# Three raw windows instead of two, an earlier start of the edge gathers, and another pace of the expert work

## The chip, the cores and the metric

The kernel runs on one core of a Trainium2 chip. The metric is the device time of one execution in microseconds (us); the median of three runs before the change is 1178.66 us (1176.34 to 1180.91). The engines are TensorE (PE, with its weight loads as PEld), VectorE (DVE), ScalarE (ACT), GpSimd (POOL) and SyncE (SP). Each works through its own queue in the order of the program and waits at semaphores for the others. DMAs are issued from the queues of SP, ACT and POOL.

## What is computed

A graph layer and a mixture of experts over 6250 nodes of 256 numbers, with 100000 edges sorted by their target:

```python
x = x + gnn(layernorm(x), stack([src, dst]), W, b)
x = x + ffn(layernorm(x)[None], ...)[0]

# gnn
msg_sum = segment_sum(h[src], dst)
deg = segment_sum(ones, dst)
return concat([h, msg_sum / maximum(deg, 1)], 1) @ W.T + b

# ffn: two of eight experts for every node
xn = layernorm(x) * gamma + beta
w = softmax over the two largest of xn @ Wr + br
for e in range(8):
    h = gelu(xn @ W1[e] + b1[e])
    y += (h @ W2[e] + b2[e]) * w[e]
```

## The kernel before

**Two products ahead of the edges.** W has two halves. The z part (`z_block`, 13 blocks of four node tiles) multiplies the normalized nodes by the half for neighbours and stores z in DRAM (`z_d`); eight more columns carry the router. The own half, u, is made in 25 steps (`u_stages`, two node tiles each) later, between edge tiles, and is stored in `u_d`.

**The edge loop.** The edges are cut into 56 windows (W) of 14 tiles (C) of 128 edges; t = 14 g + c counts the 784 edge tiles. `gather` (L646) is an indirect DMA on POOL's queue: 128 rows of z into one of 28 buffers `xg` (XG). `add_edges` (L665) multiplies seven tiles at a time (HC) by one-hot matrices `hot` into the PSUM tile pS, of which there is one; the two halves of its partitions take every second tile. It is called at c = 6 and c = 13, and the gathers for the tile 28 further on follow it, since they reuse the buffers. So a gather needs the matmul of the tile 28 before it.

**Raw windows.** The first two windows (RAW) do not wait for z. `gather_raw` (L345) loads the source indices `src_i` on SP and gathers rows of x itself; `raw_statistics`, `raw_deviations` (DVE) and `scale_raw` (ACT, L329) normalize them, seven tiles at a time; after the sum `take_raw_sums`, `turn_raw_sums` and `multiply_raw_sums` copy, transpose and multiply the window's sums by the weights. `gather_raw` is called at the sixth block of z. What else is to be done in the z part stands in the list `steps`, two entries a block from the fourth block on. Window 0's first half is normalized there; its edges are added in the edge loop at t = 0 and 7. Window 1 is normalized at t = 2 and t = 15.

**A window's end.** `window_done` (L1062) sets by tile counts what follows: `keep_sums` copies pS (ACT, L692), which frees it for the next window; `merge_sums` (PE, L696) makes pX; `window_x1` (DVE) divides by the degree and adds u, which `load_u` fetches by a load on SP at a row that a register holds. For the last window, whose rows would run over the end of u_d, `load_last` (L707) fetches u by an indirect DMA on POOL, with indices from `place_tail`. Four windows make a group: it is normalized, routed, sorted by expert and planned, with offsets in tiles from the classes Steps, LateSteps and LastSteps. The plan (which rows of y_d belong to a node) is stored by `put_plan` on SP.

**Experts.** 60 tiles after a group's end (36 and 29 in the late ones) its expert tasks are ready: per pair of experts two `hidden` steps counted as 2.0 us and two `result` steps counted as 1.75 us, 30 us for a group. `after` (L1133) lets out so much of them per edge tile: 0.72, in the last 56 tiles 0.6, after the edges 1.2 or 2.0. Three batches of 8, 5 and 1 groups (BATCHES) have 8, 5 and 2 spare tiles (`more_stages`) for tokens beyond an expert's slots.

**The end.** When a batch is complete, `gather_rows` loads x1 on SP and gathers each node's two rows of y_d on POOL, into the same 28 buffers; `add_rows` (DVE, L1031) weighs and adds them and stores the result from SP. These gathers stand behind all edge gathers on POOL.

Everything is in an order that the program writes out (`manual_schedule`): no engine reorders it.

Of the kernel before, what the change touches and what calls it, by code (L numbers as in the profile page):

```python
# [8 lines left out]
F32 = mybir.dt.float32  # L9
I32 = mybir.dt.int32  # L10
# [13 lines left out]
CAP = 64  # L24
BATCHES = (8, 8), (5, 5), (1, 2)
GB = 3
LATE = 40
XG = 28
RAW = 2
LATE_CHUNKS = 4  # L30
# [3 lines left out]
def gnn_ffn_kernel(ctx: ExitStack, tc: tile.TileContext, x, x_cols, src, dst, dst_next, gw, gw_t, gb, gb_cols, gamma, beta,  # L34
# [73 lines left out]
    z_d = dram.tile([HR, DZ], F32, name="z_d")  # L108
    u_d = dram.tile([HR, DZ], F32, name="u_d")
    y_d = dram.tile([batches[-1].end_row, D], F32, name="y_d")  # L110
# [59 lines left out]
    dst_i = u_pool.tile([P, W, C], I32, name="dst_i", bufs=1)  # L170
    xg = [edges.tile([P, DA], F32, name=f"xg{i}") for i in range(XG)]

    def constants():
        for g in xg:
            nc.vector.memset(g[:, D:DZ], 0.0)
            nc.vector.memset(g[:, DZ:], 1.0)
        nc.vector.tensor_scalar(before, ej, 0.0, None, op0=ALU.is_lt)
        nc.scalar.activation(cols, coli, AF.Copy)
        nc.vector.tensor_copy(lane, lanei)
        nc.vector.tensor_scalar(upper, col, lane, None, op0=ALU.is_gt)  # L180
        nc.vector.tensor_scalar(second, lane, HALF - 0.5, None, op0=ALU.is_gt)
        nc.vector.scalar_tensor_tensor(lane_of, second, -float(HALF), lane, op0=ALU.mult, op1=ALU.add)
# [135 lines left out]
    def raw_statistics(some):  # L318
        for t in some:
            statistics(mv_e[:, t, :], xg[t][:, :D])  # L320

# [5 lines left out]
    def scale_raw(some):  # L327
        for t in some:
            nc.scalar.activation(xg[t][:, :D], xg[t][:, :D], AF.Identity, scale=rstd_e[:, t:t + 1])  # L329

# [11 lines left out]
    def load_edges():  # L342
        nc.sync.dma_start(dst_i, dst)

    def gather_raw():  # L345

        nc.sync.dma_start(src_i, src)
        for t in range(RAW * C):
            nc.gpsimd.indirect_dma_start(  # L349
                out=xg[t][:, :D], out_offset=None, in_=x[:, :],  # L350
                in_offset=bass.IndirectOffsetOnAxis(ap=src_i[:, t // C, t % C:t % C + 1], axis=0))
# [18 lines left out]
    ends = edges.tile([P, W], F32, name="ends")  # L370
    tail_i = edges.tile([P, 1], I32, name="tail_i")
    wrongs = const.tile([1, 1], F32, name="wrongs")
# [27 lines left out]
    def place_edges():  # L400
# [4 lines left out]
            [P, W, HC, 2]), op=ALU.subtract)  # L405

    def place_tail():
        tail_f = early.tile([P, 1], F32, name="tail_f", bufs=1)
        nc.vector.tensor_tensor(tail_f, bases[:, 0, W - 1:W], lane, op=ALU.add)
        nc.vector.tensor_scalar(tail_f, tail_f, float(N - 1), None, op0=ALU.min)  # L410
        nc.vector.tensor_copy(tail_i, tail_f)

# [84 lines left out]
    hot_first = u_pool.tile([P, C, HALF], F32, name="hot_first", bufs=1)  # L497
    zero = u_pool.tile([CAP, D], F32, name="zero", bufs=1)

    def clear_first():  # L500
        nc.vector.memset(zero, 0.0)
        nc.vector.memset(states, 0.0)

    def make_hot(hot, g, c):
        nc.vector.tensor_tensor(hot, cols[:, None, :HALF].to_broadcast([P, HC, HALF]),  # L505
                                rel[:, g, c:c + HC, None].to_broadcast([P, HC, HALF]), op=ALU.is_equal)

    steps = [[constants], [lambda: placed_rows.append(place_windows())], [lambda: router_columns(0)],
             [lambda: spread_windows(placed_rows[0])], [lambda: wide_b.append(router_biases())],
             [lambda: center_weights(0)], [place_rows, place_tail], [lambda: add_biases(wide_b[0])], [place_edges],  # L510
             [lambda: make_hot(hot_first[:, :HC], 0, 0)], [check_windows], [lambda: make_hot(hot_first[:, HC:], 0, HC)], [],
             [clear_first], [some(raw_statistics, 0, 3)],
             [some(raw_statistics, 3, 2)], [some(raw_statistics, 5, 2), lambda: raw_deviations(0, HC)],
             [some(scale_raw, 0, HC), some(raw_statistics, HC, 3)], [some(raw_statistics, HC + 3, HC - 3)]]
    router_weights()
# [15 lines left out]
    for t0 in blocks:  # L531
        if t0 + 4 * TB in blocks:
            load_block(t0 + 4 * TB)
        if t0 == blocks[5]:
            gather_raw()
        z_block(t0, steps if t0 >= blocks[3] else None)
    assert not ahead
    assert not steps
    raw_deviations(HC, C - HC)
    scale_raw(range(HC, C))  # L540
    u_tasks = u_stages()
# [9 lines left out]

    loads = [(b1_sb, b1), (b2_sb, all_rows(b2, [[D, NX], [1, D]]))]

# [92 lines left out]
    def gather(g, c):  # L646
        nc.gpsimd.indirect_dma_start(  # L647
            out=xg[(g * C + c) % XG][:, :DZ], out_offset=None, in_=z_d[:, :],
            in_offset=bass.IndirectOffsetOnAxis(ap=src_i[:, g, c:c + 1], axis=0))
# [7 lines left out]
    def merge_tiles(V):  # L657
# [3 lines left out]
        if V.g > 0:  # L661
            V.carry = work.tile([P, HALF], F32, name="carry")
            nc.vector.tensor_scalar(V.carry, cols[:, :HALF], 0.0, ends[:, V.g - 1:V.g], op0=ALU.is_equal, op1=ALU.mult)

    def add_edges(V, first, last):  # L665
        if first == 0:
            V.pS = ps.tile([P, DA], F32, name="pS", bufs=1)
        halves = V.pS[:HALF, :], V.pS[HALF:, :]
        for c in range(first, last):
            nc.tensor.matmul(halves[c % 2], V.hot[c // HC][:, c % HC, :], xg[(V.g * C + c) % XG],  # L670
                             start=(c < 2), stop=(c >= C - 2 and (c % 2 == 1 or V.g == 0)))
        if last == C and V.g > 0:
            nc.tensor.matmul(halves[0], V.carry, V.before.raw if V.g < RAW else V.before.sums, start=False, stop=True)  # L673

# [23 lines left out]
    def load_u(V):  # L698
        if V.g < W - 1:
            V.x1 = work.tile([P, DZ], F32, name="x1", bufs=CW)  # L700
            nc.sync.dma_start(V.x1, u_d[window_rows(V.g), :])
        else:
            V.x1 = u_last

    u_last = edges.tile([P, DZ], F32, name="u_last")

    def load_last():  # L707
        nc.gpsimd.indirect_dma_start(
            out=u_last, out_offset=None, in_=u_d[:, :],
            in_offset=bass.IndirectOffsetOnAxis(ap=tail_i, axis=0))  # L710

# [298 lines left out]
    def spare():  # L1010

        nonlocal spares
        spares += 1
        return xg[(W * C + spares - 1) % XG][:, :D]

# [25 lines left out]
    class Steps:  # L1041

        x1, var, roots, norms, route, exps, weigh, choices, count = 3, 5, 7, 9, 11, 14, 15, 16, 19
        hot, sort = (22, 24, 26, 28), (26, 28, 30, 32)
        runs, rest, place, tiles, copied, rows, pace, start, apart = 30, 33, 36, 39, 40, 46, 1.5, 60, 2

    class LateSteps:

        x1, var, roots, norms, route, exps, weigh, choices, count = 3, 4, 5, 7, 9, 11, 12, 13, 15
        hot, sort = (17, 18, 20, 22), (19, 21, 23, 25)  # L1050
        runs, rest, place, tiles, copied, rows, pace, start, apart = 20, 22, 24, 27, 26, 28, 1.25, 36, 1

    class LastSteps:

        x1, var, roots, norms, route, exps, weigh, choices, count = 3, 4, 5, 6, 7, 8, 9, 10, 12
        hot, sort = (13, 14, 17, 18), (15, 16, 19, 20)
# [5 lines left out]
    def window_done(V, G, K, t):  # L1062
# [10 lines left out]
        at(t + more, keep_sums, V)  # L1073
        at(t + more + S.x1 - 1, merge_sums, V)
        at(t + S.x1 + more, window_x1, V)
# [57 lines left out]
    def after(t):  # L1133
# [6 lines left out]

        pace = 0.6 if W * C - 56 <= t < W * C else 0.72 if t < W * C else 1.2 if len(Ks) < W // CW else 2.0
        spent = min(spent + pace, pace) if tasks else 0.0
# [7 lines left out]
    def new_window(g, V_before):  # L1150
        V = Group()
        V.g, V.before, V.hot = g, V_before, []
        if g == 0:
            V.hot = [hot_first[:, :HC], hot_first[:, HC:]]
        else:
            hot_tiles(V, 0)
        merge_tiles(V)
        return V

    def groups(g):  # L1160

        if g == 0:
            return {0: (0, HC), HC: (HC, C)}
        if g == W - 1:
            return {HC - 1: (0, HC), C - 4: (HC, C - 3), C - 1: (C - 3, C)}
        return {HC - 1: (0, HC), C - 1: (HC, C)}

    now = 0
    V = new_window(0, None)
    edge_tiles = [(g, c) for g in range(W) for c in range(C)]  # L1170
    for g, c in edge_tiles[RAW * C:XG]:
        gather(g, c)
# [3 lines left out]
    for index in range(W // CW):  # L1176
# [10 lines left out]
        for g in range(K.first, K.first + CW):  # L1187
            if g > 0:
                V = V_next
            for c in range(C):  # L1190
# [5 lines left out]
                if c == 0 and g > 0:  # L1196
                    hot_tiles(V, HC)
                if t in (2, C + 1):
                    some_raw = range(C, C + HC) if t == 2 else range(C + HC, 2 * C)
                    raw_statistics(some_raw)  # L1200
# [4 lines left out]
                if some_edges:  # L1205
                    for g_c in edge_tiles[g * C + some_edges[0] + XG:g * C + some_edges[1] + XG]:
                        gather(*g_c)
                for to, what in loads[:1]:
                    loads.pop(0)
                    nc.sync.dma_start(to, what)  # L1210
                if u_tasks and t >= HC and t % 3 == 0:
                    u_tasks.pop(0)()
                    if not u_tasks:
                        u_pools.close()
                        slots = fast_pools.enter_context(tc.tile_pool(name="slots", bufs=2))
                        at(t + 60, load_last)
                        xe = slots.tile([P, KD, SC], F32, name="xe", bufs=1)
# [168 lines left out]
```

## Time and profile before

| What | us |
|---|---|
| median of three runs | 1178.66 |
| the profiled execution | 1180.93 |
| its span (first to last instruction) | 1178.8 |
| first raw gather on POOL | 46.5 |
| last store of z issued on SP | 72.4 |
| last edge gather starts | 1031.4 |
| last gather of y_d starts | 1166.1 |

The table by stretches of the trace (us; busy time and instructions of each engine, granted clock of PE, share of the 16 DMA engines, GB/s):

```profile
30.00:60.00 30.00, 28.09 (x133) 23.24 (x131) 26.20 (x128) 11.47 (x28) 10.48 (x11) 1.00 1.00 391
120.00:150.00 30.00, 27.63 (x144) 18.40 (x144) 21.10 (x63) 2.27 (x4) 22.99 (x24) 1.00 0.86 272
500.00:600.00 100.00, 86.80 (x503) 62.12 (x504) 48.49 (x198) 41.40 (x116) 75.64 (x81) 0.97 0.55 138
1050.00:1100.00 50.00, 37.99 (x127) 26.77 (x128) 33.72 (x119) 20.64 (x65) 31.40 (x33) 0.83 0.66 174
```

The five figures with an x are PE, PEld, DVE, ACT and POOL. In a timeline a row gives the start, the duration, the engine and line, the operation with its output and inputs, how often, and in brackets how long the engine sat idle before it and what ended that. A queue's row (SPq) is the issue of a DMA, not its transfer.

### The profile page before, as it was taken

The page shows a single profiled execution, that of the slowest core. Times are in us where ns is not written, and L with a number is a line of the kernel's source. Part 1 is how long each engine was busy: PE and PEld are TensorE (multiplying, and loading weights), DVE is VectorE, ACT ScalarE, POOL GpSimd, SP SyncE. Part 2 cuts the span into 40 slices and gives each one's busy share as a digit, 9 for nine tenths or more (in the row PEclk, how much of TensorE's full clock was granted, in tenths as well). Part 3 has the DMA queues.
Part 4 walks back from the last instruction along what each step waited for, and adds up shares of the span by engine and source line. Part 5 has one row for each costly group of instructions (what it writes and reads, how often), then busy time and mean ns, then how long its engine had stood idle before and what let it go on. Part 6 is the DMA issues. An engine that isn't in the chain of part 4 may idle for free. (4 is left out here: it accounts for less than half of the span.)

```text
span 1178.8 us, 19193 instructions
## 1 busy us (share of the span) xinstructions
PE 973.3 (83%) x5470; PEld 717.0 (61%) x5470; DVE 650.6 (55%) x2530; ACT 477.2 (40%) x1305; POOL 845.1 (72%) x892
## 2 busy tenths in 40 slices
PE   7967974897989788897979889899889989888960
PEld 5745652776757465574747567467676767665840
DVE  5887694554546364544635545374644636267442
ACT  2441017444454344445334434445364524434410
POOL 0377777777777777777777777777777777777674
PEclk9998987898989799998979979999999999989985
DMA  9988878966565655556565555755665564767784
GB/s 318 395 259 271 281 237 250 282 172 135 144 136 141 146 139 140 141 136 136 143 138 138 148 125 145 147 144 138 160 128 154 134 156 135 170 195 186 228 239 115
DMA packets 128859, 210.04 MB, mean 178 GB/s; under 512 B 36652, under 2 KB 87064, under 8 KB 128620
## 3 DMA queue, kind: packets, MB, share of 16 engines
q0 software_dynamic: 42768, 118.85, 42.3%
q1 hardware_dynamic: 77644, 80.45, 21.0%
q10 hardware_dynamic: 8336, 9.45, 2.5%
q8 instruction: 46, 0.75, 0.3%
q14 instruction: 65, 0.53, 0.1%
HBM read 163.80 MB, written 44.86 MB: 177 GB/s over the span
## 5 line engine op out<-in xcount | busy, mean ns | idle before, releaser
L647 POOL DMA_INDIRECT xg<-z_d,src_i x756 | 719.1, 951 | 230.6 <-issue 121.5
L670 PE MATMUL pS<-xg,hot 128*64 128x265 f32 x1540 | 267.6, 417 | 54.9 <-DMA xg<-z_d,src_i 54.4
L932 PEld LDWEIGHTS ph<-xe,w_sb 128*128 128x128 f32 x1792 | 223.4, 202 | 15.4 <-issue 9.2
L932 PE MATMUL ph<-xe,w_sb 128*128 128x128 f32 x1792 | 228.6, 287 | 2.3 <-ACT xe L905 2.3
L670 PEld LDWEIGHTS pS<-xg,hot 128*64 128x64 f32 x1540 | 122.8, 142 | 172.6 <-DMA xg<-z_d,src_i 95.5
L945 PE MATMUL py<-w_sb,hid 128*128 128x256 f32 x896 | 219.1, 392 | 9.7 <-DVE rows L949 6.1
L945 PEld LDWEIGHTS py<-w_sb,hid 128*128 128x128 f32 x896 | 168.0, 193 | 50.0 <-issue 16.8
L937 ACT ACTIVATE hid<-ph,b_sb 128x128 f32<-128x128 f32 x448 | 127.1, 368 | 141.4 <-PE ph L932 141.1
L905 ACT ACTIVATE xe<-xs x448 | 139.4, 311 | 77.5 <-ACT xe L905 37.6
L949 DVE TENSOR_TENSOR rows<-py,b_sb 128x512 f32<-128x512 f32 x56 | 38.6, 689 | 169.6 <-PE py L945 168.1
L1024 POOL DMA_INDIRECT xg<-y_d,plans x98 | 97.1, 991 | 38.4 <-issue 16.8
L764 ACT ACTIVATE xs<-pm,beta_sb,gamma_sb 128x256 f32<-128x256 f32 x112 | 57.1, 568 | 112.4 <-PE pm L761 112.4
L696 PE MATMUL pX<-sums,merge 128*128 128x265 f32 x112 | 41.7, 457 | 51.5 <-ACT sums L692 51.5
L714 DVE TENSOR_SCALAR rdeg<-pX 128x1 f32<-128x1 f32 x56 | 8.6, 153 | 134.9 <-PE pX L696 134.9
L692 ACT ACTIVATE sums<-pS 128x265 f32<-128x265 f32 x56 | 21.7, 388 | 139.2 <-PE pS L673 133.7
L505 DVE TENSOR_TENSOR hot<-cols,rel 128x448 f32<-128x448 f32 x110 | 67.3, 612 | 10.0 <-PE pS L670 10.0
L349 POOL DMA_INDIRECT xg<-x_dram,src_i x28 | 26.7, 954 | 52.8 <-DMA src_i<-src_dram 44.6
L281 PE MATMUL ph<-gc,x_t 128*128 128x264 f32 (+1 forms) x200 | 58.3, 416 | 6.4 <-ACT zt L305 3.5
L761 PE MATMUL pm<-to,xn 128*128 128x256 f32 x224 | 58.6, 393 | 5.7 <-DVE to L754 3.5
L1031 DVE SCALAR_TENSOR_TENSOR xg<-xg,plans,xg 128x256 f32<-128x256 f32 (+1 forms) x98 | 46.4, 483 | 28.3 <-DMA xg<-y_d,plans 26.8
L696 PEld LDWEIGHTS pX<-sums,merge 128*128 128x128 f32 x112 | 20.3, 206 | 66.8 <-ACT sums L692 65.1
L937 ACT ACT_TABLE_LOAD x25 | 32.1, 1283 | 62.1 <-PE ph L932 57.6
(229 smaller groups left out, 1069.4 us busy)
## 6 DMA issues: line engine op xcount, KB each, us to landing
y_d<-rows SPq DMA_DIRECT2D x56, 256.0 KB
xg<-z_d,src_i POOLq DMA_INDIRECT x756, 3.3
w_sb<-w_dram ACTq DMA_DIRECT2D x16, 512.0 KB
x<-u_d SPq DMA_DIRECT2D x55, 132.0 KB
x_d<-x SPq DMA_DIRECT2D x55, 128.0 KB
u_d<-u_t SPq DMA_DIRECT2D x24, 264.0 KB
x_t<-x_cols_dram SPq DMA_DIRECT2D x12, 512.0 KB
xu<-x_dram SPq DMA_DIRECT2D x24, 256.0 KB
```

What stands on the lines that cost most here:

```text
L281: nc.tensor.matmul(pz, x_t[:, t, k, :], gc[:, h * KD + k, :n], start=(k == 0), stop=(k == KD - 1))
L505: nc.vector.tensor_tensor(hot, cols[:, None, :HALF].to_broadcast([P, HC, HALF]), rel[:, g, c:c + HC, None].to_broadcast([P, HC, HALF]), op ...
L647: nc.gpsimd.indirect_dma_start(out=xg[(g * C + c) % XG][:, :DZ], out_offset=None, in_=z_d[:, :], in_offset=bass.IndirectOffsetOnAxis(ap=sr ...
L670: nc.tensor.matmul(halves[c % 2], V.hot[c // HC][:, c % HC, :], xg[(V.g * C + c) % XG], start=(c < 2), stop=(c >= C - 2 and (c % 2 == 1 or ...
L696: nc.tensor.matmul(V.pX, V.merge, V.sums, start=True, stop=True)
L761: nc.tensor.matmul(px[:, k, :], G.xn[i][:, k * P:(k + 1) * P], G.one_hot[i], start=True, stop=True)
L764: nc.scalar.activation(xs[:, at:at + 2 * P], px[:, k, :], AF.Identity, bias=beta_sb[:, k:k + 1], scale=gamma_sb[:, k:k + 1])
L905: nc.scalar.activation(xe[:, :, bass.ds(to_at, CAP)], src[:, :, bass.ds(src_at, CAP)], AF.Copy)
L932: nc.tensor.matmul(ph[:, i, a * SH:(a + 1) * SH], w1_sb[:, U.e + a, k, c * P:(c + 1) * P], xe[:, k, at:at + SH], start=(k == 0), stop=(k = ...
L937: nc.scalar.activation(U.hid[:, c, a * SH:(a + 1) * SH], ph[:, i, a * SH:(a + 1) * SH], AF.Gelu, bias=b1_sb[:, U.e + a, c:c + 1])
L945: nc.tensor.matmul(U.py[:, h, :], U.hid[:, c, h * P:(h + 1) * P], w2_sb[:, U.e + h, c, :], start=(c == 0), stop=(c == KH - 1))
L1024: nc.gpsimd.indirect_dma_start(out=V.y2[r], out_offset=None, in_=y_d[:K.batch.end_row, :], in_offset=bass.IndirectOffsetOnAxis(ap=plans[:c ...
```

## The change

- RAW is 3: 42 raw tiles. They need 42 buffers: 14 more (`third`) lie in the pool of the u part. `rows_for` gives a tile's buffer: the first 28 tiles and all from tile 42 on use the 28 buffers, tiles 28 to 41 use `third`.
- `gather_raw` is called at the third block of z (`blocks[2]`) and loads only the first three windows' indices; the other 53 follow at the eighth block (`load_sources`).
- All 14 tiles of window 0 are normalized and summed in the z part: `add_edges` stands in `steps`, twice. The check of the windows moves behind it.
- In the edge loop windows 1 and 2 are normalized at t = 2, 15, 23 and 29. The first 14 gathers of z (window 3) are issued at the start; windows 0 and 2 are followed by none, window 1 by those of tiles 56 to 69; from window 3 on it is 28 tiles ahead again.
- The expert pace is 0.95 on all edge tiles, and the middle batch has 4 spare tiles for 5.
- `merge_sums` has an offset of its own, one tile later than before except in the last group.
- u_d has 128 more rows, which are cleared, so the last window loads its u on SP like all others. `place_tail` and `load_last` are gone.
- The buffers are one tile, and its constant columns are set by four wide memsets in place of 56.

```diff
-BATCHES = (8, 8), (5, 5), (1, 2)
+BATCHES = (8, 8), (5, 4), (1, 2)
-RAW = 2
+RAW = 3
...
+    def rows_for(t):
+        if XG <= t < RAW * C:
+            return third[:, t - XG, :]
+        return xg[(t if t < XG else t - RAW * C) % XG]
...
+    def load_sources():
+        nc.sync.dma_start(src_i[:, RAW:], src[:, RAW:])
...
-        nc.sync.dma_start(src_i, src)
+        nc.sync.dma_start(src_i[:, :RAW], src[:, :RAW])
...
-             [lambda: make_hot(hot_first[:, :HC], 0, 0)], [check_windows], [lambda: make_hot(hot_first[:, HC:], 0, HC)], [],
-             [clear_first], [some(raw_statistics, 0, 3)],
-             [some(raw_statistics, 3, 2)], [some(raw_statistics, 5, 2), lambda: raw_deviations(0, HC)],
-             [some(scale_raw, 0, HC), some(raw_statistics, HC, 3)], [some(raw_statistics, HC + 3, HC - 3)]]
+             [lambda: make_hot(hot_first[:, :HC], 0, 0)], [lambda: make_hot(hot_first[:, HC:], 0, HC)],
+             [some(raw_statistics, 0, 4)], [some(raw_statistics, 4, HC - 4), lambda: raw_deviations(0, HC)],
+             [some(scale_raw, 0, HC), some(raw_statistics, HC, 2)],
+             [lambda: add_edges(V_first, 0, HC), some(raw_statistics, HC + 2, 3)],
+             [some(raw_statistics, HC + 5, C - HC - 5), lambda: raw_deviations(HC, C - HC)],
+             [some(scale_raw, HC, C - HC), clear_first], [lambda: add_edges(V_first, HC, C), check_windows], []]
...
-        if t0 == blocks[5]:
+        if t0 == blocks[2]:
             gather_raw()
+        if t0 == blocks[7]:
+            load_sources()
...
-        at(t + more + S.x1 - 1, merge_sums, V)
+        at(t + more + S.merge, merge_sums, V)
...
-        pace = 0.6 if W * C - 56 <= t < W * C else 0.72 if t < W * C else 1.2 if len(Ks) < W // CW else 2.0
+        pace = 0.95 if t < W * C else 1.2 if len(Ks) < W // CW else 2.0
...
+    raw_at = {2: C, C + 1: C + HC, C + HC + 2: 2 * C, 2 * C + 1: 2 * C + HC}
...
-                if t in (2, C + 1):
-                    some_raw = range(C, C + HC) if t == 2 else range(C + HC, 2 * C)
+                if t in raw_at:
+                    some_raw = range(raw_at[t], raw_at[t] + HC)
...
-                    for g_c in edge_tiles[g * C + some_edges[0] + XG:g * C + some_edges[1] + XG]:
-                        gather(*g_c)
+                    ahead = XG if g >= RAW else RAW * C if g * C < XG else None
+                    if ahead:
+                        for g_c in edge_tiles[g * C + some_edges[0] + ahead:g * C + some_edges[1] + ahead]:
+                            gather(*g_c)
...
-                        at(t + 60, load_last)
```

## The prediction

> **What bounds the kernel now.** First the busy times, then GpSimd's (POOL's) timeline, since the issue time between slices is not counted as busy.
>
> ```profile
> PE 973.3 (83%) x5470; PEld 717.0 (61%) x5470; DVE 650.6 (55%) x2530; ACT 477.2 (40%) x1305; POOL 845.1 (72%) x892
> ```
>
> PE looks fullest. POOL's timeline (start, duration, line, idle before it and releaser) says otherwise:
>
> ```profile
> 46.47 1.13 POOL L349 DMA_INDIRECT xg<-x_dram,src_i  x1 [44.62 <-DMA src_i<-src_dram]
> 47.91 0.98 POOL L349 DMA_INDIRECT xg<-x_dram,src_i  x1 [0.31 <-issue]
> ...
> 172.82 0.94 POOL L647 DMA_INDIRECT xg<-z_d,src_i  x1 [0.30 <-DMA xg<-z_d,src_i]
> ...
> 1031.43 0.95 POOL L647 DMA_INDIRECT xg<-z_d,src_i  x1 [0.30 <-issue]
> 1032.68 0.95 POOL L1024 DMA_INDIRECT xg<-y_d,plans  x1 [0.30 <-issue]
> ...
> 1086.63 0.94 POOL L1024 DMA_INDIRECT xg<-y_d,plans  x1 [1.00 <-DVE of L838]
> 1087.88 0.94 POOL L1024 DMA_INDIRECT xg<-y_d,plans  x1 [0.30 <-issue]
> 1091.49 0.94 POOL L1024 DMA_INDIRECT xg<-y_d,plans  x1 [2.67 <-DMA out_dram<-xg]
> 1092.74 0.95 POOL L1024 DMA_INDIRECT xg<-y_d,plans  x1 [0.30 <-issue]
> 1099.50 0.94 POOL L1024 DMA_INDIRECT xg<-y_d,plans  x1 [5.82 <-DVE xg L1031]
> ```
>
> A gather takes 0.95 us and the next starts 0.30 after it: pitch 1.25. From 46.47 to 1032.68 stand 785 gathers (784 tiles, one last u); 785 x 1.25 = 981 of 986 us. POOL never waits for a buffer there. Then come 98 gathers of y_d (122 us) with a hole at 1085 to 1099 (0.70 + 2.37 + 5.52 = 8.6 us over the usual 0.30), and 12.7 us from the last gather's start (1166.1) to the end. So the end moves with POOL's chain. Gather n+28 needs the buffer of tile n, so I looked for how far PE is ahead of that, in PE's timeline:
>
> ```profile
> 98.27 3.13 PE L670 MATMUL pS<-xg,hot 128*64 128x265 f32 x14
> 114.39 2.00 PE L670 MATMUL pS<-xg,hot 128*64 128x265 f32 x14
> 126.43 2.00 PE L670 MATMUL pS<-xg,hot 128*64 128x265 f32 x14
> 167.04 2.88 PE L670 MATMUL pS<-xg,hot 128*64 128x265 f32 x14
> ```
>
> These are the first matmuls of tiles 14, 28, 42 and 70. Tile 70 at 167.0 frees the buffer for gather 98, at 172.8: slack 5.8 us; for tile 42 it is 10.0 (gather 70 starts at 136.4), from tile 168 on 20 to 28. Here PE does not wait for gathers (tile 70's ended 30 us earlier); it waits for DVE and ACT:
>
> ```profile
> 75.27 0.11 DVE L639 MEMSET xs<- 128x64 f32 x1 [0.86 <-DMA z_d<-zt]
> ...
> 75.53 0.42 DVE L201 BATCH_NORM_STATS2 st<-xg 128x6 f32<-128x256 f32 x1
> 75.98 0.18 DVE L202 BATCH_NORM_AGGREGATE mv_e<-st 128x2 f32<-128x6 f32 x1
> ...
> 80.71 0.17 DVE L196 TENSOR_TENSOR rstd_e<-rstd_e,newton 128x7 f32<-128x7 f32 x1
> ```
>
> Seven raw tiles hold DVE 5.4 us (75.5 to 80.9), and ACT 2.9 us to scale them (L329). The raw part of a window is dear on DVE, not on POOL.
>
> **The change, part by part.** *Earlier raw gathers.* The first src load stands on SP behind the loads of block 6 (x_t issued at 22.95) instead of 36.38. From issue to first gather took 9.2 us (37.23 to 46.47); the same again gives a start at 23.4 + 9.2 = 32.6, 13.9 us earlier. 42 raw gathers then last to 85.1, by which time z lies in DRAM (below: 79.6), so POOL goes on without a hole up to gather 56.
>
> In 30 to 60 us the table by stretches shows a DMA share of 1.00 at 391 GB/s. Eleven gathers of 131 KB brought forward are 1.44 MB, 3.7 us at that rate, by which the x loads of the z part may come later. I take 0 for it, since DVE's only wait for an x tile after 25 us is 0.79 and the loads run four blocks ahead; 3.7 is the upper bound. A rule speaks against the change here: the Trainium skill (DMA: Bandwidth & Descriptors, Issuing engines are not separate DMA queues) says that the DMAs of all issuers interleave on the same 16 engines, so that a transfer from POOL takes from one of SP; by it the 3.7 would be paid in full, and the sum below would end 3.7 higher, at 1190.
>
> *Window 0 inside the z part.* DVE's work from the first hot tiles (51.56) to the second raw deviations (74.3) is 22.7 us. Without the window check and the clears (2.9), moved behind it, 19.9 remain, begun 1.4 earlier (1.0 of memsets made wide, 0.4 of the tail): 70.0. Then in order: scale 2.9 on ACT, 14 edge matmuls 2.0, the last z product 0.9, its scale 0.5: 76.3, against 72.4. The store took 2.9 to free DVE's first instruction of the main loop: 79.2, and with hand-overs of 0.1 each 79.6, 4.3 later.
>
> *Third raw window: two more DVE blocks of 5.4.* From 75.3 to 93.7 DVE ran 18.5 us of things that stay, so window 1's second statistics end at 98.1; scale 2.9 and copy 0.4 free the PSUM: window 1 starts on PE at 101.7 (was 98.3). Its edges 3.1, merge 0.6, four u products 3.7, second edges 1.9: 111.0. Now a new wait: the instruction order puts the first scaling of window 2 ahead of the copy of window 1's sums on ACT. DVE: two u steps at 1.8, hot and merge tiles 1.2, u after its products (107.9), x1 1.5, statistics 5.4: 114.8; ACT 2.9 + 0.4: 118.1. Behind the copy on PE stand the transposes and all that follows. DVE: two u steps and hot tile 4.2, statistics 5.4: 124.4; scale and the keep of window 1 (queued behind it): 127.8. Window 2 starts at 127.9 (was 114.4). Then edges 1.9, merge 0.6, four products 3.7, edges 1.9, u 1.9, transposes, copy and multiply 1.9, u 1.9: tile 42 at 141.7, 15.3 late. From tile 42 to 70 PE took 40.6, set by u stores and the first routing on DVE; nothing there becomes shorter: tile 70 at 182.3.
>
> So the 13.9 us gained are lost again at gather 70 (142 instead of 136.4), and gather 98 goes at 182.4 instead of 172.8: **+9.6**. Bounds: below, DVE without a pause from 79.6 has 51 us ahead of tile 42's u products (four raw blocks 21.6, eleven u steps 19.8, hot tiles, checks and two x1 9.6): 131, 4.6 late, within tile 70's slack of 5.8, so 0; above, 3.7 for the x loads and 2 for hand-overs that I have cut too short, +15.3.
>
> *Expert pace 0.95 for 0.72.* In the first group the new order has four expert steps of 1.9 us more ahead of tile 140: 7.6. Tile 140: 248.5 + 15.3 + 7.6 = 271.4; gather 168 is ready at 261.6 + 9.6 - 1.25 (the last u's gather, gone from in front of it) = 270.0. **+1.5**, and **-1.25** for the u gather. The load takes 0.35 on SP and adds its zeroes in a 0.4 us issue, both beside POOL. Later groups have 20 us of slack against 8. Bounds 0 and +4.
>
> *Tail.* Group 12's experts get 0.95 for 0.6 in the last 20 tiles, 7 us, and one spare tile (4 us) is gone, so 11 us less is left for after the edges, and the y_d stores no longer stand between the plan stores on SP. But SP still makes four plan stores of 3 to 5 us each, one behind another, while x1 loads and out stores queue there, and POOL needs their buffers. Of the hole's 8.6 us I take **-2.5** (near the DVE wait of 5.8 halved); bounds -8.6 and +2.
>
> *At nothing:* merges one step later (PE fills the time with u or experts; its cover is POOL's chain) and the wide memsets.
>
> Sum against the execution's span: 1178.8 + 9.6 + 1.5 - 1.25 - 2.5 = 1186.2. That run took 1180.9 around its span; the median of three is 1178.7, so the shift of 7.4 gives **1186**.
>
> **Rivals.** (1) *The head start is kept or the tail hole closes*: PE would have to reach tile 70 by 167 and the hole go: 1178.7 - 1.25 - 8.6 = 1169; with all 13.9 kept as well, 1155. For it: POOL's solid chain. Against: 5.8 us of slack and 10.8 us more of DVE. It ends faster. (2) *Break-even*: DVE stays dense, so that gather 98 is 4 late, tail -4: 1178. For it: DVE waits of 1 to 2 us on u_d stores that the lateness hides. (3) *Expert pace takes over*: PE per tile while experts run, 0.95 x 1.07 (448 us of expert matmuls for 14 x 30) + 0.52 = 1.53 against 1.25; 33 tiles a group lose 9 us. If PE never won its lag back, each of 13 groups would stop POOL: up to +117, some 1215 if three do. It decides from a lag over 28 tiles. Against: the slack of 20 us and the same expert total. (4) *It does not do what it says*: the mean expert work per tile cannot rise by a third, since a group's total stays; only its place moves, as counted above.
>
> **Chances.** Forecast 0.53, (2) 0.28, (1) 0.13, (3) 0.06. About 0.5% (5.9 us) is what can be told from no change. Faster 0.13, same 0.28, slower 0.59. All lower bounds together give 1168.8, all upper ones 1198.7; the range, 1171 to 1199, leaves out the corner of (1) and most of (3). The forecast's own is 1181 to 1196.
>
> **What would show it.** First gather at 32 to 34; no POOL wait up to gather 56; then idle of about 20 us before the gather of tile 70; tile 42's matmul near 142, tile 70's near 182; gather 98 near 182; the last edge gather near 1041; the hole in the tail 4 to 8 us. Wrong if POOL's timeline has no such idle, or if DVE reaches the third window's statistics before 105.

## The result, and the profile after

| | before | after |
|---|---|---|
| median of four runs, us | 1179.63 | 1210.79 |
| ratio, 95% interval | | 1.026 (1.0224 to 1.0297) |
| span of the profiled run | 1178.8 | 1208.2 |
| first raw gather on POOL | 46.47 | 33.20 |
| matmul of tile 28 / 42 / 70 starts | 114.4 / 126.4 / 167.0 | 127.7 / 141.6 / 179.8 |
| gather 98 starts | 172.8 | 181.2 |
| last edge gather starts | 1031.4 | 1041.6 |
| last edge matmul starts | 1035.5 | 1070.8 |
| from the last edge matmul to the end | 143.3 | 137.4 |

The forecast was 1186, with 1171 to 1199 as its range; the changed kernel takes 1211, 25 us more. Up to the last edge gather the table follows the forecast within 3 us; the loss lies behind it. Some of the sets of experiments below fell on chips where the kernel of before itself takes 1474 to 1484 us; each ratio is against the kernel of before on the same chip, and for each set the time of that kernel is given.

The busy times of the changed kernel's page:

```profile
PE 974.1 (81%) x5460; PEld 727.2 (60%) x5460; DVE 658.8 (55%) x2513; ACT 479.6 (40%) x1316; POOL 844.9 (70%) x891
```

The two fullest engines have no more to do than before (PE 973.3, POOL 845.1), and DVE, busy for 55% of the span, has 8.2 us more: 29 us of span have come without work that would account for them. POOL's timeline of the changed kernel (start, duration, line, idle before it and releaser) shows where the early part goes:

```profile
33.20 1.13 POOL L361 DMA_INDIRECT gathered<-x_dram,src_i  x1 [31.36 <-DMA src_i<-src_dram]
...
121.07 0.95 POOL L669 DMA_INDIRECT gathered<-z_d,src_i  x1 [0.30 <-issue]
142.54 1.28 POOL L669 DMA_INDIRECT gathered<-z_d,src_i  x1 [20.52 <-PE pS L519]
...
181.23 0.95 POOL L669 DMA_INDIRECT gathered<-z_d,src_i  x1 [2.18 <-PE pS L519]
...
1041.63 0.94 POOL L669 DMA_INDIRECT gathered<-z_d,src_i  x1 [0.30 <-issue]
...
1046.63 0.95 POOL L1026 DMA_INDIRECT gathered<-y_d,plans  x1 [0.30 <-issue]
1052.76 0.94 POOL L1026 DMA_INDIRECT gathered<-y_d,plans  x1 [5.18 <-PE pS L519]
```

It starts 13.3 us earlier and then stands 20.5 us, waiting for the matmul of tile 42, so gather 98 is 8.4 us late. From there to the last edge gather it runs nearly without a stop (two waits over 0.5 us, of 1.4 and 1.2; +10.2 at 1041.6). The last row is the new thing: behind the edges POOL waits for PE's edge matmuls, since PE is still 28 tiles back. PE's timeline of the changed kernel, tiles 28, 42 and 70 and the last edge tile:

```profile
127.66 1.56 PE L519 MATMUL pS<-third,hot 128*64 128x265 f32 x12 [2.11 <-ACT sums L704]
...
141.61 1.56 PE L519 MATMUL pS<-gathered,hot 128*64 128x265 f32 x12
...
179.82 1.42 PE L519 MATMUL pS<-gathered,hot 128*64 128x265 f32 x6
...
1070.76 0.39 PE L519 MATMUL pS<-gathered,hot 128*64 128x265 f32 x1
```

and the same last edge tile in the kernel of before:

```profile
1035.49 0.39 PE L670 MATMUL pS<-xg,hot 128*64 128x265 f32 x1
```

The last window is summed 35.3 us later, though its rows were asked for only 10.2 later: PE's lag, the start of a tile's matmul less the start of its gather, is 29.1 us at the last tile for 4.1 before. Then normalization, routing, planning and the experts of the last group must follow; that part is 5.9 us shorter than before, and 35.3 - 5.9 = 29.4 is the whole difference of the spans.

### The profile page after: what moved, and what is told of

It reads as the page before. It is cut to its first block, busy times and chain, and to the rows that moved or that the text cites. A ratio compares the mean times of both kernels' runs of the same rounds, so it can differ in the third digit from the quotient of the medians.

```text
span 1208.2 us, 19130 instructions
## 1 busy us (share of the span) xinstructions
PE 974.1 (81%) x5460; PEld 727.2 (60%) x5460; DVE 658.8 (55%) x2513; ACT 479.6 (40%) x1316; POOL 844.9 (70%) x891
## 4 chain that ended last, share of the span: by engine, by line
PE 53%; DVE 18%; DMA 12%; ACT 8%; issue 5%; ACTq 2%; POOL 1%; SPq 0%; POOLq 0%; DVEq 0%
PE ph L934 16%; PE py L947 14%; PE pS L519 10%; ACT xe L907 6%; DMA gathered<-z_d,src_i 5%; PE pm L763 3%; DMA plan_d<-plan 2%; DVE st L209 2%; PE ph L977 2%; PE pX L708 2%; DMA gathered<-y_d,plans 2%; PE ph L289 1%; ACTq L896 1%; DVE rows L951 1%; PE py L995 1%
## 5 line engine op out<-in xcount | busy, mean ns | idle before, releaser
L669 POOL DMA_INDIRECT gathered<-z_d,src_i x742 | 706.1, 952 | 250.2 <-issue 132.8
L519 PE MATMUL pS<-gathered,hot 128*64 128x265 f32 x1512 | 258.8, 434 | 36.8 <-DMA gathered<-z_d,src_i 31.3
L934 PE MATMUL ph<-xe,w_sb 128*128 128x128 f32 x1792 | 233.9, 291 | 24.9 <-ACT xe L907 22.1
L934 PEld LDWEIGHTS ph<-xe,w_sb 128*128 128x128 f32 x1792 | 229.8, 206 | 39.1 <-ACT xe L907 24.4
L519 PEld LDWEIGHTS pS<-gathered,hot 128*64 128x64 f32 x1512 | 124.0, 149 | 149.1 <-DMA gathered<-z_d,src_i 59.6
L939 ACT ACTIVATE hid<-ph,b_sb 128x128 f32<-128x128 f32 x448 | 126.4, 371 | 180.7 <-PE ph L934 177.4
L907 ACT ACTIVATE xe<-xs x448 | 139.3, 311 | 99.7 <-ACT xe L907 37.2
L1026 POOL DMA_INDIRECT gathered<-y_d,plans x98 | 97.0, 989 | 57.7 <-issue 16.5
L1033 DVE SCALAR_TENSOR_TENSOR gathered<-gathered,plans 128x256 f32<-128x256 f32 (+1 forms) x98 | 45.7, 482 | 20.2 <-DMA gathered<-y_d,plans 18.7
L361 POOL DMA_INDIRECT gathered<-x_dram,src_i x28 | 27.1, 968 | 39.6 <-DMA src_i<-src_dram 31.4
L289 PE MATMUL pm<-gc,x_t 128*128 128x264 f32 (+1 forms) x192 | 54.5, 409 | 0.0
L763 PEld LDWEIGHTS pm<-to,xn 128*128 128x128 f32 x224 | 41.2, 195 | 21.8 <-PE pS L519 5.6
```

Source lines behind the costliest of these rows:

```text
L289: nc.tensor.matmul(pz, x_t[:, t, k, :], gc[:, h * KD + k, :n], start=(k == 0), stop=(k == KD - 1))
L669: nc.gpsimd.indirect_dma_start(out=rows_for(g * C + c)[:, :DZ], out_offset=None, in_=z_d[:, :], in_offset=bass.IndirectOffsetOnAxis(ap=src ...
L763: nc.tensor.matmul(px[:, k, :], G.xn[i][:, k * P:(k + 1) * P], G.one_hot[i], start=True, stop=True)
L907: nc.scalar.activation(xe[:, :, bass.ds(to_at, CAP)], src[:, :, bass.ds(src_at, CAP)], AF.Copy)
L934: nc.tensor.matmul(ph[:, i, a * SH:(a + 1) * SH], w1_sb[:, U.e + a, k, c * P:(c + 1) * P], xe[:, k, at:at + SH], start=(k == 0), stop=(k = ...
L939: nc.scalar.activation(U.hid[:, c, a * SH:(a + 1) * SH], ph[:, i, a * SH:(a + 1) * SH], AF.Gelu, bias=b1_sb[:, U.e + a, c:c + 1])
```

## The experiments

Two theories were set against each other. P: the pace 0.95 makes PE late at the last edges, and the raw part costs its 8 us only. R: the raw part and the later merges cost it all.

**The pace put back.** The changed kernel with the old line:

```diff
-        pace = 0.95 if t < W * C else 1.2 if len(Ks) < W // CW else 2.0
+        pace = 0.6 if W * C - 56 <= t < W * C else 0.72 if t < W * C else 1.2 if len(Ks) < W // CW else 2.0
```

> The changed kernel with the old expert pace (0.72 per edge tile, 0.6 in the last 56) and all else as changed. Theory P (the pace lets the expert queue run dry while a group is planned, PE then idles in the planning waits and falls 28 tiles behind, so the last edges are summed 35 us late): the last edge matmul comes back from 1070 to 1040-1048, PE lags its gathers by 10 us or less from tile 560 on, and the end is 1182-1190, which is the 8 us of the raw part alone. Theory R (the raw part and the later merges cost it, not the pace): the end stays above 1200 and the last edge matmul above 1060.

> The changed kernel with the old expert pace, once more (the first set ran where the kernel of before took 1484 us and POOL waited for PE all along the edges). Theory P, where the kernel of before takes about 1179: 1182-1190 (ratio 1.003 to 1.010), last edge matmul at 1040-1048, PE 12 us or less behind its gathers from tile 560 on. Theory R: ratio above 1.017, last edge matmul above 1060.

> The changed kernel with the old expert pace, where the kernel of before takes 1179. Theory P: 1182-1190 (ratio 1.003 to 1.010): the raw part's 8 us stays, last edge gather at 1038-1044, last edge matmul at 1040-1048 (1073 with the changed pace), PE 14 us or less behind its gathers from tile 560 on. Theory R: ratio above 1.017, last edge matmul above 1060.

> The changed kernel with the old expert pace, where the kernel of before takes 1179 (and the changed one 1211). Theory P: 1182-1190 (ratio 1.003 to 1.010): the raw part's 8 us stays, last edge gather at 1038-1044, last edge matmul at 1040-1048 (1073 with the changed pace), PE 14 us or less behind its gathers from tile 560 on. Theory R: ratio above 1.017, last edge matmul above 1060. On a chip where before takes 1480: ratio 1.006 to 1.014 as in the three runs there.

Where before takes 1181 (the fourth run): 1188.1 us, ratio 1.0062 (1.0041 to 1.0082). Where it takes 1484, 1478 and 1474: 1.0071 (1.0033 to 1.0109), 1.0128 (1.002 to 1.0236) and 1.0078 (1.0015 to 1.0141). POOL's timeline of the fourth run:

```profile
142.67 1.28 POOL L669 DMA_INDIRECT gathered<-z_d,src_i  x1 [21.07 <-PE pS L519]
...
181.48 0.95 POOL L669 DMA_INDIRECT gathered<-z_d,src_i  x1 [2.18 <-PE pS L519]
...
1040.90 0.95 POOL L669 DMA_INDIRECT gathered<-z_d,src_i  x1 [0.30 <-PE pS L519]
```

and its last edge tile on PE:

```profile
1045.18 0.39 PE L519 MATMUL pS<-gathered,hot 128*64 128x265 f32 x1
```

The hole of the raw part is there as in the changed kernel, and the edge gathers end at the same time; but PE ends 4 us behind POOL and not 29. So the raw part and everything else but the pace cost 7 us (0.62%), and the pace the rest, 22 us or so: theory R falls.

**The pace alone.** The kernel of before with the line `pace = 0.95 if t < W * C else 1.2 ...`:

> The kernel of before with the expert pace 0.95 on all edge tiles and nothing else changed. Theory P: the edge gathers stay where they were (last one at 1031 +- 3), but PE lags them by 20 us or more from tile 560 on, the last edge matmul comes at 1050-1062 instead of 1035, and the end is 1195-1206. Theory R: within 5 us of before (1174-1184).

> The kernel of before with the pace 0.95 and nothing else, once more. Theory P, where the kernel of before takes about 1179: last edge gather at 1031 +- 3, expert matmuls bunched (160 and 32 in turn per 28 tiles, for 128 and 64), PE idle in the planning waits, last edge matmul at 1050-1062, end 1195-1206 (ratio 1.014 to 1.023). Theory R: ratio 0.996 to 1.004.

> The kernel of before with the pace 0.95 and nothing else, where the kernel of before takes 1179. Theory P: last edge gather at 1031 +- 4, last edge matmul at 1055-1066 (1034 before), end 1196-1206 (ratio 1.014 to 1.023). Theory R: ratio 0.996 to 1.004.

All three fell where before takes 1484, 1478 and 1474: ratios 1.0257 (1.018 to 1.0334), 1.0343 (1.02 to 1.0485) and 1.0318 (1.0233 to 1.0404). R expected 1.000. The positions along the edges that P gave did not come about there, since on those chips POOL waits for PE all along (see the last section).

**The kernels themselves on one chip.** No edit:

> The kernel of before itself, to have its trace from the chips of the experiments. If these are like the two sets so far: ratio 1.000, a span near 1480, POOL waiting for PE all along the edges, a group of 56 tiles 82-85 us long with 20-23 us of idle PE (70.2 and 9.7 in the recorded run).

> The changed kernel itself. If the pace is the larger part on these chips too: ratio to before 1.035 to 1.055, that is pace95_alone's 1.026-1.034 plus pace_back's 1.007-1.013; a group of 56 tiles 88-91 us long with 26-29 us of idle PE. If the parts do not add up (raw part and pace hide each other): ratio below 1.03.

Here before takes 1180: 1178.5 us, ratio 0.9991 (0.9973 to 1.0008), and the changed kernel 1210.8, ratio 1.0245 (1.0219 to 1.0271). The expectations had been made for the other chips and their numbers miss; the recorded result is repeated. Whether the costs of the pace and of the raw part simply add up stays open, since 0.95 by itself was not run where before takes 1180. What PE waited for from tile 532 to the last edge (total, times, longest, all in us), first in this run of before, then in this run of the changed kernel:

```profile
PE pS L670 <- DMA xg<-z_d,src_i: 11.8, 16, 1.6
PE pX L696 <- ACT sums L692: 9.4, 7, 3.1
PE ph L975 <- ACT xe L905: 4.5, 2, 2.9
PE pm L761 <- DVE to L754: 1.7, 1, 1.7
PE pm L734 <- DVE both L728: 1.1, 2, 0.7
```

```profile
PE pX L708 <- ACT sums L704: 17.2, 3, 5.9
PE ph L934 <- ACT xe L907: 8.6, 3, 3.7
PE ph L934 <- ACT hid L939: 5.1, 1, 5.1
PE ph L977 <- ACT xe L907: 4.7, 3, 2.4
PE pm L763 <- DVE to L756: 4.4, 2, 2.2
PE pm L736 <- DVE both L730: 3.9, 2, 2.0
```

Before, PE's first wait is for gathers: it is level with POOL and has time to spare. After, it never waits for a gather; it waits for the steps by which ACT and DVE plan the next group, in fewer but longer waits. In this stretch PE needs 331.2 us for 307.9: 7.0 more of busy time for nearly the same matmuls, and 16.3 more idle (47.9 for 31.6). The table by stretches has it, before and after; the granted clock is 0.93 for 0.99:

```profile
726.80:1034.70 307.90, 276.25 (x1674) 203.56 (x1672) 155.76 (x614) 143.46 (x413) 232.95 (x247) 0.99 0.58 146
```

```profile
742.20:1073.40 331.20, 283.27 (x1687) 213.44 (x1688) 156.18 (x613) 142.82 (x415) 242.27 (x256) 0.93 0.56 140
```

Why these waits stand bare is seen by counting the records of expert matmuls (hidden, result and spare tiles) on PE per 28 edge tiles, in the profiled runs of the first table:

| edge tiles | before | after |
|---|---|---|
| 616 to 643 | 112 | 160 |
| 644 to 671 | 128 | 176 |
| 672 to 699 | 144 | 16 |
| 700 to 727 | 112 | 176 |
| 728 to 755 | 104 | 16 |

The same work, bunched: at 0.95 a group's experts are used up before the next plan begins, and PE has nothing to put into its waits. By 56 tiles, before_here and then after_here in each cell (us; lag at the end of the stretch):

| edge tiles | length | expert matmuls | PE idle | lag |
|---|---|---|---|---|
| 504 to 559 | 72.9, 82.6 | 196, 240 | 8.0, 6.4 | 13.2, 24.3 |
| 560 to 615 | 66.5, 67.9 | 220, 240 | 3.8, 7.0 | 9.6, 22.1 |
| 616 to 671 | 68.6, 82.6 | 240, 336 | 6.8, 6.8 | 8.1, 34.4 |
| 672 to 727 | 68.2, 72.1 | 256, 192 | 5.8, 13.8 | 6.3, 35.7 |
| 728 to the last | 66.5, 64.1 | 192, 144 | 9.8, 14.3 | 4.0, 28.8 |

So the lag has two parts. It grows by 12 us or so in each of two stretches in which more expert work is let out than PE has time for, with no more idle time than before; and it is hardly won back where there is less of that work, since there PE idles 28.1 us for 15.6. One place of the second kind in the changed kernel, on PE and on ACT:

```profile
955.61 1.78 PE L519 MATMUL pS<-gathered,hot 128*64 128x265 f32 x13
...
963.60 1.25 PE L708 MATMUL pX<-sums,merge 128*128 128x265 f32 x2 [5.65 <-ACT sums L704]
964.78 3.79 PE L519 MATMUL pS<-gathered,hot 128*64 128x265 f32 x14
972.29 7.49 PE L934 MATMUL ph<-xe,w_sb 128*128 128x128 f32 x48 [3.72 <-ACT xe L907]
979.71 1.78 PE L519 MATMUL pS<-gathered,hot 128*64 128x265 f32 x13
```

```profile
958.40 1.34 ACT L907 ACTIVATE xe<-xs  x4 [1.66 <-DVE of L840]
960.16 1.34 ACT L907 ACTIVATE xe<-xs  x4 [0.42 <-ACT xe L907]
961.93 1.34 ACT L907 ACTIVATE xe<-xs  x4 [0.42 <-ACT xe L907]
963.17 0.37 ACT L704 ACTIVATE sums<-pS 128x265 f32<-128x265 f32 x1
```

The copy of the window's sums (L704) stands on ACT behind three runs of expert slots (L907); PE's merge waits 5.65 us for it. And what follows the wait runs at half speed: 14 records of edge matmuls (the trace has two for each tile) take 3.79 us at 964.78, but 13 take 1.78 before the wait and 1.78 again later. The granted clock says the same, in the table by stretches from 940 to 980, after and before:

```profile
940.00:980.00 40.00, 26.02 (x132) 17.21 (x130) 22.53 (x99) 18.34 (x52) 29.81 (x32) 0.74 0.57 132
```

```profile
940.00:980.00 40.00, 35.51 (x212) 26.81 (x212) 13.06 (x42) 12.14 (x36) 30.26 (x32) 0.96 0.60 150
```

0.74 for 0.96 (the figure behind POOL's). From 300 us to the last edge, PE has no idle stretch over 3.4 us in before, in its second run and with the pace put back, but 8 in the changed kernel and 9 in its second run. The Trainium skill (TensorE: Matmul & The Clock Gate, Part 1: The HAM clock gate) says that the array falls to half its clock after an idle window of some 3.4 us and needs as long of busy time to come back; the rows agree with that: 0.27 us a record behind a wait of 5.65 us, 0.14 otherwise. They show no sharp border at 3.4 us, though: in before the granted clock is 0.50 from 162 to 167 us, behind two waits of 3.13 and 3.15 us, and 1.00 from 867 to 871, behind one of 3.07.

**Where in the group it hurts.** The kernel of before with 0.95, and each group's experts let out 14 tiles later in all but the last four groups:

```diff
-        runs, rest, place, tiles, copied, rows, pace, start, apart = 30, 33, 36, 39, 40, 46, 1.5, 60, 2
+        runs, rest, place, tiles, copied, rows, pace, start, apart = 30, 33, 36, 39, 40, 46, 1.5, 74, 2
```

> pace95_alone with the experts of a group started 74 tiles after its end instead of 60 (all but the last four groups). Theory P1: PE's idle time moves with the hole in the expert work: in tiles 35 to 41 of a group, where expert matmuls now stand, it falls from 8 us to under 3, and in tiles 0 to 13, now without any, it rises from 2 to over 4. Theory P2 (0.95 of expert work per tile is more than PE has time for, wherever it stands): idle in tiles 35 to 41 stays above 6 and the stretch with experts stays 12 us long per 7 tiles; the end within 1% of pace95_alone's ratio (1.026-1.034).

1197.2 us, ratio 1.0134 (1.011 to 1.0157), on the chip of the two runs above. Means over six groups (tiles 224 to 559), idle time of PE in us and expert matmuls in brackets:

| tiles of the group | before_here | after_here | phase74 |
|---|---|---|---|
| 0 to 13 | 1.1 (64) | 0.2 (88) | 6.1 (32) |
| 35 to 41 | 1.0 (8) | 3.3 (3) | 0.8 (32) |
| length of a group | 70.7 | 71.7 | 71.1 |

The idle time goes where the expert work isn't, as P1 had it, with other numbers than on the chips for which they were given. But here five of the six groups take 67 to 72 us in all three runs, hardly other than POOL's 56 x 1.25 = 70: what is lost in one half is won back in the other. The sixth (504 to 559) takes 72.9, 82.6 and 82.7; there, as in the table above, what P2 says fits, more expert work than PE has time for. In the late groups (560 to 727), whose experts follow sooner and which have the spare tiles besides, it is 67.8 before, 74.2 after, 74.8 in phase74 and 68.0 with the pace put back: more than 70, and the lag grows. The gathers of phase74 are those of before (the last at 1032.2), its last edge matmul is at 1058.8, and it ends 20 us later than before_here. Its last edge matmul:

```profile
1058.78 0.39 PE L670 MATMUL pS<-xg,hot 128*64 128x265 f32 x1
```

So 0.95 with the later start of the experts, and nothing of the raw part, costs this where before takes 1180, with no stop of POOL along the edges after 101 us. The two were not taken apart there; the late groups, which keep their start, show the growth of the lag.

**More even than before.**

```diff
-        pace = 0.6 if W * C - 56 <= t < W * C else 0.72 if t < W * C else 1.2 if len(Ks) < W // CW else 2.0
+        pace = 0.6 if t < 8 * CW * C or W * C - 56 <= t < W * C else 0.72 if t < W * C else 1.2 if len(Ks) < W // CW else 2.0
```

> The kernel of before with pace 0.6 instead of 0.72 in the first 448 edge tiles. Theory P1 (what hurts is that expert work is bunched, so PE has nothing to do while a group is planned; the more even, the better): where before takes 1480, a group of 56 tiles gets shorter by 3 to 6 us (PE idle down by as much), ratio 0.975 to 0.995; where before takes 1179, PE closer to its gathers and the same time within 4 us. Theory P2 (any pace under some limit is as good; 0.95 is over it): the group's length within 1 us of before's, ratio 0.997 to 1.003.

1179.2 us, ratio 0.9982 (0.9967 to 0.9998): no difference that counts; PE lags its gathers by 4.9 us for 5.9 (mean of tiles 224 to 447). With before at 1180 this does not part P1 from P2: POOL sets the length there.

**Which tiles.** The kernel of before with 0.95 from tile 504 on; and the changed kernel with 0.6 in the last 56 tiles:

```diff
+        pace = 0.95 if 504 <= t < W * C else 0.72 if t < W * C else 1.2 if len(Ks) < W // CW else 2.0
```

```diff
+        pace = 0.6 if W * C - 56 <= t < W * C else 0.95 if t < W * C else 1.2 if len(Ks) < W // CW else 2.0
```

> The kernel of before with the pace 0.95 from edge tile 504 on only (the batch of the first eight groups ends there, and the late groups with their shorter times follow). If the harm of the pace is done there: last edge matmul at 1055-1066 and a ratio of 1.014 to 1.023, as with 0.95 on all tiles. If it is carried along from the first groups: last edge matmul below 1045 and a ratio below 1.008.

> The changed kernel with pace 0.6 in the last 56 edge tiles only, 0.95 before them. If what hurts is only that PE cannot catch up in the last 56 tiles: 1183-1192, last edge matmul below 1050. Theory P (the lag is built up from tile 560 on, group by group, and cannot be won back in 56 tiles): 1198-1208, last edge matmul at 1058-1068, lag at tile 728 still above 30 us.

> The changed kernel with pace 0.6 in the last 56 edge tiles only, 0.95 before them, once more. If what hurts is only that PE cannot catch up in the last 56 tiles: ratio to before 1.003 to 1.010, last edge matmul below 1050. Theory P (the lag is built up group by group from tile 532 on and cannot be won back in 56 tiles): ratio 1.016 to 1.025, lag at tile 728 still above 28 us, last edge matmul at 1056-1068.

All where before takes 1474 to 1484. late95: 1.0149 (1.0064 to 1.0235), half of what 0.95 on all tiles costs on the same chip (1.0318). The expected place is right in part: on such chips PE is behind from the start, and the early groups seem to cost as well (the two intervals meet at 1.0234). With 0.6 in the last 56 tiles: 1.0448 (1.0356 to 1.054) and 1.0532 (1.0384 to 1.0679), far from the 1.003 to 1.010 of the first case, so the catch-up at the end alone was not what was missing, and above the 1.016 to 1.025 of theory P, which misses too; the changed kernel itself was not run on those chips, so that is as far as it goes.

**The raw part.** The changed kernel with the old pace and the third raw window left unnormalized (its statistics, deviations and scaling are left out, its sums are of plain rows); and the changed kernel with the old pace and two raw windows:

```diff
-                if t in raw_at:
+                if t in raw_at and raw_at[t] < 2 * C:
```

```diff
-RAW = 3
+RAW = 2
...
-    raw_at = {2: C, C + 1: C + HC, C + HC + 2: 2 * C, 2 * C + 1: 2 * C + HC}
+    raw_at = {2: C, C + 1: C + HC}
```

> As the first kernel of this set (old pace), with the third raw window left unnormalized: its statistics, deviations and scaling are left out, so its sums are those of plain rows. If the 10.8 us of DVE (and 5.8 us of ACT) for that window hold up the edges: tile 42's matmul comes at 129-133 instead of 141.6, POOL's hole before the gather of tile 70 shrinks from 20 to 8-12 us, gather 98 goes at 168-174, and the end is 8-12 us below the first kernel's (1172-1179). If it is the order of the raw windows on PE and ACT (copy, transposes, second product) that holds them: hole of 17 us or more, and an end within 3 us of the first kernel's.

> The changed kernel with two raw windows and the old pace: what remains is the early start, window 0 summed in the z part, the plain u load, the later merges, one spare tile less. If the third raw window's DVE work is what holds up the edges: no hole over 3 us in POOL's gathers up to gather 98, which goes at 170-176 (172.8 before, 181.2 changed); last edge gather 1029-1034; end 1174-1181, 6 to 10 us below pace_back_2. If it is the sums in the z part or the early gathers: gather 98 at 178 or later and an end within 3 us of pace_back_2.

> The changed kernel with two raw windows and the old pace, where the kernel of before takes 1179. If the third raw window's DVE work is what holds up the edges: no hole over 3 us up to gather 98, which goes at 168-176; last edge gather 1027-1034; end 1172-1181, 6 to 12 us below pace_back_3. If it is the sums in the z part or the early gathers: gather 98 at 178 or later and an end within 3 us of pace_back_3.

> The changed kernel with two raw windows and the old pace. Where the kernel of before takes 1179: if the third raw window's DVE work is what holds up the edges, no hole over 3 us in POOL's gathers up to gather 98, which goes at 168-176 (181.2 changed); last edge gather 1027-1034; ratio 0.993 to 1.002, that is 6 to 12 us below pace_back_4 (1.0062). If it is the sums in the z part or the early gathers: gather 98 at 178 or later and a ratio of 1.004 to 1.008. On a chip where before takes 1480: 0.99 to 1.006 as in the two runs there.

None of the four fell where before takes 1180, so the rows that were to tell (gather 98, POOL's hole) can't be held against the expected numbers: POOL waits there from its first gathers of z on. Unnormalized: 1.0026 (0.9991 to 1.0062), pace_back on the same chip 1.0071; tile 42 came 4.4 us earlier, not 9 to 12. Two raw windows: 1.0045 (1.0000 to 1.0090), 0.9951 (0.9899 to 1.0003) and 0.9994 (0.9936 to 1.0051), below pace_back on the same chip in both sets that had both (1.0128, 1.0078). The intervals of the first pair overlap. On that chip gather 98 goes at 228.1 with two raw windows and at 242.3 with three; unnormalized, on its own chip, it goes at 243.7 for 244.9. That the third window is the costly one of the raw part is thus supported; that its normalization is, is not. Both stay open where before takes 1180. No version beat the kernel of before by more than 0.5%, and of the gains only pace60's 0.2% lies outside its interval.

## Why the prediction was wrong

Point by point, with the run of the changed kernel, and of the pace put back (the fourth) where it tells more:

- *Earlier raw gathers*: 32.6 was forecast, 33.2 came, and no wait up to gather 56 beyond 0.5 us. The x loads that might come later did not: DVE had no wait for an x tile from 25 to 75 us (0.8 before). The 3.7 us that the prediction estimated by the Trainium skill's rule on shared engines (DMA: Bandwidth & Descriptors, Issuing engines are not separate DMA queues) were not seen.
- *Window 0 in the z part*: the main loop's first DVE instruction at 79.6, measured 79.1. Window 1 on PE at 101.7, measured 100.7.
- *Third raw window*: window 2 at 127.9, tile 42 at 141.7, tile 70 at 182.3, gather 98 at 182.4 (+9.6); measured 127.7, 141.6, 179.8 and 181.2 (+8.4). The sum over DVE, ACT and PE held to within 2.5 us over 100 us of work.
- *Expert pace*: +1.5 at gather 168, measured nothing (269.1 against 270.0). That term was near for gather 168 and wrong as a price of the edit, with bounds of 0 and +4: it measured 22 us or so (1210.8 us with the edit and 1188.1 without, on chips where before takes 1180 and 1181).
- *The u gather*: -1.25; with the pace put back gather 98 is 8.7 late and the last edge gather 9.5, so it does not show; where it went is open.
- *Tail*: -2.5. With the pace put back, last edge gather to end is 145.1 for 147.4, so -2.3; but before_here, with no edit, has 145.3, so this agreement may be chance. With the changed pace it is 166.6: +19.2.

The step that failed is "Later groups have 20 us of slack against 8", with the sentence that the end moves with POOL's chain. The slack was counted as what may be lost before POOL stops, as if lag that stops no gather were free; and the 8 were too few, since the lag grows from 11.7 us at tile 504 to 35.7 at 728 (after_here). It is not free, at the end: the last window must be summed before the last group can be planned, so PE's lag at the last tile is added to the end, whether POOL ever waited or not; only the 4 to 6 us of expert work that no longer stand behind the edges come off. The runs show it over 39 us (start of the last edge matmul, end of span, difference):

| run | last edge matmul | end | difference |
|---|---|---|---|
| before_here | 1034.7 | 1175.7 | 141.0 |
| kernel of before | 1035.5 | 1178.8 | 143.3 |
| pace60 | 1036.1 | 1177.0 | 140.9 |
| pace_back_4 | 1045.2 | 1186.0 | 140.8 |
| phase74 | 1058.8 | 1195.7 | 136.9 |
| changed kernel | 1070.8 | 1208.2 | 137.4 |
| after_here | 1073.4 | 1210.7 | 137.3 |

The 0.6 of the last 56 tiles was in the kernel of before, and PE's lag of 4.1 us at the last tile in its trace; both were there to be read. The tail's other half, 11 us less work behind the edges, was right in kind and too large: 4 to 6 us.

Rival 3 had named the mechanism (PE's time per tile over POOL's pitch, the lag never won back); its 1.53 us per tile is near the 82.6 / 56 = 1.48 of tiles 616 to 671. That its 1215 lies 4 us from the result is luck, since it stands for three groups that stop POOL for 9 us each, and behind gather 98 POOL's longest stops along the edges are 1.4 and 1.2 us. It got 0.06 since its price was put only on stops of POOL and since the expert total is the same. The total is the same indeed; but it came where PE had no time for it, and where it was missing PE's idle and half-speed time rose, because the evenly spread experts were what filled its waits. The size of the raw part was right: without the pace term the forecast's sum is 1184.7, and the run with the pace put back spans 1186.0 (the sum still holds the -2.5 of the tail, part of which was owed to the new pace).

## What to carry to other kernels

A buffer's slack tells when a lagging consumer stops its producer; it does not tell what the lag costs at the end, where all that waits for the last item is late by it. So follow both chains to the last instruction, the producer's and the consumer's. Work that is spread between other work is a filler for waits: letting it out faster moves no total, but it makes the consumer late in one place and leaves waits bare in another, and on TensorE a bare wait long enough costs the clock as well.

## What was not expected of the hardware

**Waits that halve TensorE's speed in an otherwise full kernel.** Nine PE waits of 3.6 to 5.9 us in some 770 us go with a granted clock of 0.890 over the whole span (after_here); six go with 0.908 (phase74), none with 0.918, 0.927 and 0.937 (pace_back_4, before_here, pace60).

**Chips on which the same program takes a quarter longer.** On four of the six chips of the experiments the kernel of before took 1474 to 1484 us. Busy times of POOL and DVE are alike (844.2 and 659.1 us on the page of pace_back, 846.7 and 659.1 in its fourth run), PE's is 1034.7 for 969.5 at a granted clock of 0.84 for 0.92, and whole engines stand still for what the records don't name. In the second run of pace_back, in DVE's timeline and in the list of PE's waits from 300 to 700 us:

```profile
90.89 0.17 DVE L271 COPY gb_r<-py 128x8 f32<-128x8 f32 x1 [45.01 <-remote]
```

```profile
PE pX L708 <- issue: 70.7, 5, 15.7
```

The copy that waits 45 us here starts at 43.9 in the fourth run of the same kernel. In that run the instruction queue brings blocks at 53.1, 56.5 and 63.0 us; in the second it brings none between 32 and 97. That the engines wait for their code there fits these rows; no run was made to test it. The pace costs on both kinds of chip: 2.6 to 3.4% by itself there, 1.8% here (1.0245 with it and 1.0062 without), though along the edges POOL waits for PE on the one kind and sets the length on the other.
